# Moving the product with ones behind a burst's scores, in a group norm and attention kernel

## Chip, core and metric

The kernel runs on one core of one Trainium2 chip. The metric is the device time of one execution in microseconds, the median of a few runs. A profile is one further execution, recorded instruction by instruction.

## What is computed

The input x is 4 images of 512 channels and 48 by 48 = 2304 positions. The reference, cut to what matters:

```python
hn = _group_norm(x, gn_scale, gn_bias)                    # 32 groups of 16 channels
qkv = einsum('oc,bchw->bohw', qkv_w, hn) + qkv_b          # 1536 rows, then float16
q, k, v = ...                                             # 8 heads of 64 channels
w = softmax(einsum('bhct,bhcs->bhts', q * scale, k * scale), axis=-1)
a = einsum('bhts,bhcs->bhct', w, v)
return x + einsum('oc,bchw->bohw', proj_w, a) + proj_b
```

## The kernel before, in words

**Engines.** TensorE (PE) does all products, ScalarE (ACT) the exponentials, VectorE (DVE) evacuates PSUM and adds up the exponentials, GpSimd (POOL) divides by the sums, SyncE (SP) issues nearly all DMAs. Each works through its instructions in the order in which the program issues them, and the program fixes that order by hand: the loop at line 1355 calls small functions, and each call puts its instructions at the end of the queues of the engines concerned.

**Bursts and blocks.** Heads are worked in pairs, 4 pairs an image, 16 in all. A pair's 2304 query positions are cut into blocks: four of 512 and one of 256. A block against all 18 tiles of 128 key positions is cut into bursts of three exponential tiles (`stream`, line 935): 6 bursts for a block of 512, 3 for one of 256, so 27 a pair and 432 in all. There are 80 blocks, so 80 block ends.

**One burst, one turn of the loop.** In turn n the loop issues: the scores of burst n (`scores`, line 943: matmuls of k and q into a PSUM tile `ps`, and the exponential of each into `p`; there are three `ps` tiles, so a tile's scores wait for the exponential of the tile three before); the add of burst n-1's exponentials into `acc` (`add`, line 991; at a block's last burst two further adds fold the three thirds of `acc` into one); the values of burst n-2 (`values`, line 965: matmuls of v and p into `av`); and `fill` (line 1306).

**What fills the gaps.** `fill` issues work of other stages: statistics and normalization of the next image (`tasks`, on DVE), and pieces of chains (`beside`, on PE): chains for q and k (`pqk`, line 695), for v (`pv`, line 743) and for the output projection (`pr`, line 840). A planner gives each piece a cost and a due time, and a credit per turn decides how many are issued. All chains share one PSUM bank (`pw`), so a chain's first matmul waits until DVE has evacuated the chain before it.

**A block's end.** Let the block's last burst be e. In turn e+2, after `values` of e, DVE copies `av` to `avx` (line 989), and then comes `fill`. In turn e+3:

- loads that are due are issued (`loads`, a queue of functions with the turn from which they are due: stores of finished projections, the residual loads two chains ahead, and reloads of x for the next image, four tiles at a time; a projection or a reload queues them for the turn after);
- `add_up` (line 1015): two or four matmuls of `acc` with a tile of ones give the sums over keys, in the PSUM bank `sl`, which is the bank of `av` (one buffer), so they wait for the `avx` copy;
- `rows` (line 1044): DVE copies `sl` to `slx`, and SP issues two small DMAs that turn one row of each head into a tile of 128 partitions (`sums`);
- then `wanted` (line 1335), which issues pieces that the coming pair can't do without (and, if there are any, every load queued), the scores of n, the add of n-1, `fill`, and the values of e+1, whose `av` tile reuses the bank and so waits for the `slx` copy.

In turn e+4 POOL checks the sums' range (`check_sums`, line 1063), and DVE inverts them (`invert`, line 1073) after they have landed; SP sends the inverses to DRAM (`row`). In turn e+5 `spread` (line 1084) reads them back to all partitions (`ib`), and in turn e+6 POOL multiplies `avx` by `ib` into `att` (`divide`, line 1094).

The last blocks but one (`soon`, line 1349: two block ends) and the last block of all have lines of their own, from 1381 on. `load_x`'s DMA has line 512, `residual` line 811, a store line 876, the transfers of the sums line 1051. The conversion piece ahead of an image's first projection issues the first two residual loads itself, not through `loads` (`begin`, line 902).

Of the kernel before, what the change touches and what calls it, by code (L numbers as in the profile page):

```python
# [467 lines left out]
def fast_path(  # L468
# [312 lines left out]
    tasks, loads = deque(), deque()  # L781
# [161 lines left out]
    def scores(u):  # L943
        g, j, k, _ = u
        o, n = QBLOCKS[j]
        per = QB // n
        qt, kt = qk[g]
        pt = ppool.tile([P, BURST, 2, QB], F16, tag="p", name=f"p_{g}_{j}_{k}")
        for r in range(BURST):
            ps = ps_s.tile([P, 2, QB], F32, tag="ps", name=f"ps_{g}_{j}_{k}_{r}")  # L950
            for a in range(per):
                i = (k * BURST + r) * per + a
                for h in range(2):
                    rows = slice(h * D, (h + 1) * D)
                    nc.tensor.matmul(  # L955
                        ps[:, h, a * n : (a + 1) * n],
                        kt[rows, bass.ts(i, P)],
                        qt[rows, o : o + n],
                        start=True,
                        stop=True,  # L960
                    )
            nc.scalar.activation(pt[:, r], ps, AF.Exp)  # L962
        pts[u] = pt

    def values(u):
        g, j, k, last = u
        b, pr = divmod(g, NPAIR)
        o, n = QBLOCKS[j]
        per = QB // n
        pt = pts.pop(u)  # L970
        if k == 0:
            if j == 0:
                atts[g] = apool.tile([P, T], F16, tag="att", name=f"att_{g}")
            av[0] = ps_av.tile([P, QB], F32, tag="av", name=f"av_{g}_{j}")
        for r in range(BURST):
            for a in range(per):
                i = (k * BURST + r) * per + a
                for h in range(2):
                    lo = h * D
                    nc.tensor.matmul(  # L980
                        av[0][lo : lo + D, :n],
                        vv[b, pr // 2][:, i, pr % 2 * P + lo : pr % 2 * P + lo + D],
                        pt[:, r, h, a * n : (a + 1) * n],
                        start=(i == 0),
                        stop=(i == NT - 1),
                    )
        if last and u is not stream[-1]:
            avx[g, j] = work.tile([P, QB], F32, tag="avx", name=f"avx_{g}_{j}")
            nc.vector.tensor_copy(avx[g, j][:, :n], av[0][:, :n])  # L989

    def add(u):

        g, j, k, last = u
        pt = pts[u]
        if k == 0:
            acc[g, j] = [pt]
            return
        if j >= NQ - 2 and g == NG - 1 and (last or j == NQ - 1):
            acc[g, j].append(pt)
            return  # L1000
        before = acc[g, j][0]
        if k == 1:
            acc[g, j] = [
                work.tile(
                    [P, BURST, 2, QB], F16, tag="acc", bufs=1, name=f"acc_{g}_{j}"
                )
            ]
        t = acc[g, j][0]
        nc.vector.tensor_tensor(t, before, pt, ALU.add)  # L1009
        if last:  # L1010
            for r in range(1, BURST):
                nc.vector.tensor_tensor(t[:, 0], t[:, 0], t[:, r], ALU.add)  # L1012
            acc[g, j] = [t[:, :1]]

    def add_up(g, j, bank=None, more=False):


        o, n = QBLOCKS[j]
        per = QB // n
        sl = bank  # L1020
        if bank is None:
            sl = ps_av.tile([P, QB], F32, tag="av", name=f"sl_{g}_{j}")
        steps = [
            (t, r, a)
            for t in acc.pop((g, j))
            for r in range(t.shape[1])
            for a in range(per)
        ]
        for i, (t, r, a) in enumerate(steps):
            for h in range(2):  # L1030
                lo = h * D
                nc.tensor.matmul(  # L1032
                    sl[lo : lo + D, :n],
                    ones16,
                    t[:, r, h, a * n : (a + 1) * n],
                    start=(i == 0 and (g, j) not in open_sums),
                    stop=(i == len(steps) - 1 and not more),
                )
        if more:
            acc[g, j] = []  # L1040
            open_sums.add((g, j))
        return sl

    def rows(g, j, sl):

        o, n = QBLOCKS[j]
        sx = work.tile([P, QB], F32, tag="rows", name=f"slx_{g}_{j}")
        nc.vector.tensor_copy(sx[:, :n], sl[:, :n])  # L1048
        sm = small.tile([P, 2, QB // P], F32, tag="sums", name=f"sums_{g}_{j}")
        for h in range(2):  # L1050
            nc.sync.dma_start(sm[:, h, : n // P], sx[h * D : h * D + 1, :n])
        sums[g, j] = sm
        return sx
# [9 lines left out]
    def check_sums(g, j):  # L1063
        n = QBLOCKS[j][1]
        sm = sums[g, j][:, :, : n // P]
        ok = fine.rearrange("p (h i) -> p h i", h=2)[:, :, : n // P]
        for op, limit in ((ALU.is_ge, SUM_MIN), (ALU.is_le, SUM_MAX)):
            t = small.tile([P, 2, QB // P], F32, tag="in", name=f"in_{g}_{j}")
            t = t[:, :, : n // P]
            nc.gpsimd.tensor_scalar(t, sm, limit, None, op)  # L1070
            nc.gpsimd.tensor_tensor(ok, ok, t, ALU.mult)
# [234 lines left out]
    def fill(n):  # L1306

        idle = beside and beside[0][4] and not beside[0][4]()
        if ended(n - 1):
            room = 1.1 if idle else 0.0
        elif ended(n - BEHIND - 1):
            room = 1.1 if idle else 0.5
        else:
            room = 2.4 if idle else 1.1
        do_tasks(room)
        rate, work = 0.0, 0.0
        for us, _, _, _, _, _, need in beside:  # L1320
            work += us
            left = min(need * per_pair, len(stream) - 4) - n
            rate = max(rate, work / max(left, 1))
        credit[0] = min(credit[0] + rate, 4.0)
        closed = False
        while beside:
            us, _, first, last, when, after, _ = beside[0]
            if after > n or (first and closed) or (when and not when()):
                break
            if us > 0.1 and credit[0] < (0.0 if first and last else us / 2):  # L1330
                break
            issue()
            closed = closed or last

    def wanted(g):

        while any(p[6] <= g for p in beside):
            while loads:
                loads.popleft()[1]()
            while tasks:  # L1340
                tasks.popleft()[2]()
            issue()
            credit[0] = max(credit[0], 0.0)
# [7 lines left out]
    def block_at(n):  # L1351

        return stream[n][:2] if ended(n) and n not in soon else None

    for n in range(end):
        now[0] = n
        while loads and loads[0][0] <= n:
            loads.popleft()[1]()
        summed = block_at(n - BEHIND - 1)
        if summed:  # L1360
            rows(*summed, add_up(*summed))
        wanted(stream[n][0])
        scores(stream[n])
        if n > 0:
            add(stream[n - 1])
        if summed:

            fill(n)
        if n >= BEHIND:
            values(stream[n - BEHIND])  # L1370
        if block_at(n - BEHIND - 2):
            check_sums(*block_at(n - BEHIND - 2))
            invert(*block_at(n - BEHIND - 2))
        if block_at(n - BEHIND - 3):
            spread(*block_at(n - BEHIND - 3))
        if block_at(n - BEHIND - 4):

            divide(*block_at(n - BEHIND - 4))
        if not summed:
            fill(n)  # L1380
        if n - BEHIND in soon:
            g, j = stream[n - BEHIND][:2]
            sx = rows(g, j, add_up(g, j))
            if n - BEHIND == soon[1]:
                divide_here(g, j, sx, avx[g, j], nc.gpsimd)
        if n - BEHIND - 1 == soon[0]:
            check_sums(g, j)
            invert(g, j)
        if n - BEHIND - 2 == soon[0]:
            spread(g, j)  # L1390
            divide(g, j)
    g, b, j = NG - 1, B - 1, NQ - 1
    n = QBLOCKS[j][1]
# [142 lines left out]
```

## Time and profile before

| | |
|---|---|
| median of 3 runs | 1610.09 us (1609.6, 1610.09, 1612.28) |
| the profiled execution's own time | 1612.11 us |
| its span, first to last instruction | 1610.4 us |
| mean granted clock of PE | 0.997 |
| scores matmuls (line 955) | x2880, busy 356.6 us |
| values matmuls (line 980) | x2880, busy 361.5 us |
| chains of q and k (line 709) | x2464, busy 519.3 us |
| product with ones (line 1032, into sl) | x192, busy 31.0 us |
| exponentials (line 962) | x1296, mean 1025 ns |
| add of a burst (line 1009) | x270, mean 1795 ns |
| copy of sl to slx (line 1048) | x79, mean 633 ns |
| transfers of the sums (line 1051) | x158, median 2.1 us from issue to landing |

How to read the lines below: a group's line has the line of the kernel, the engine, the operation, what it writes <- what it reads, shapes and count; behind the first bar its busy time and the mean of one in ns; behind the second the engine's idle time just before its instructions and what ended it. A line in order of time begins with the start and the duration in us; instructions of one kind that follow each other are merged. "SPq" marks a DMA issue on SP. A matmul's shape "128*64" is the part of the array that it uses, rows by columns.

### The profile page before, as it was taken

Reading aid. Unit: us, or ns where it says so; the run is one execution under the profiler, and the core shown is the slowest. Engines: PE = TensorE matmul, PEld = TensorE weight load, DVE = VectorE, ACT = ScalarE, POOL = GpSimd, SP = SyncE. Lnnn points to the kernel's source line nnn. Section 1 sums busy time; section 2 is a strip of 40 time slices with the busy share of each in tenths; the row PEclk is TensorE's granted clock in tenths of the full one; section 3 lists DMA queues with packets and bytes.
Section 4 is the critical chain, followed back from the end, with each engine's and each line's share of the span. In section 5 each row is a group of like instructions: output and inputs, shape, how many; then the busy total and the mean of one; then the engine's idle time right before and its main releaser. Section 6 shows DMA issues by size and latency. Waiting matters only on the chain.

```text
span 1610.4 us, 28319 instructions
## 1 busy us (share of the span) xinstructions
PE 1582.2 (98%) x11500; PEld 694.0 (43%) x11500; DVE 1136.0 (71%) x1301; ACT 1267.1 (79%) x1360; POOL 318.9 (20%) x459
## 2 busy tenths in 40 slices
PE   7999999999999999999999999999999999999997
PEld 2533434443333534555333353355533334435554
DVE  6267668866666668986666666888666766667775
ACT  3077777888888888888887887877878888888895
POOL 1011102211121222322111121222112121222222
PEclk9999999999999999999999999999999999999999
DMA  7002020000000023511000001352100000016423
GB/s 218 5 14 66 12 65 23 18 14 11 14 18 14 9 70 119 155 53 28 14 11 18 14 12 52 99 160 83 25 14 18 14 15 11 15 31 190 123 66 127
DMA packets 94896, 82.10 MB, mean 51 GB/s; under 512 B 50852, under 2 KB 60964, under 8 KB 94756
## 3 DMA queue, kind: packets, MB, share of 16 engines
q1 hardware_dynamic: 92724, 78.35, 17.7%
q8 instruction: 92, 1.51, 0.4%
q10 hardware_dynamic: 1904, 1.84, 0.4%
q14 instruction: 48, 0.39, 0.1%
q0 software_dynamic: 128, 0.01, 0.0%
HBM read 60.70 MB, written 19.17 MB: 50 GB/s over the span
## 4 chain that ended last, share of the span: by engine, by line
PE 93%; DVE 2%; DMA 2%; issue 1%; ACT 1%; POOL 1%; SPq 0%; ACTq 0%; DVEq 0%; POOLq 0%
PE pqk L709 29%; PE ps L955 19%; PE av L980 19%; PE pv L760 16%; PE pr L844 8%; PE ps L709 1%; PE sl L1032 1%; DVE acc L1009 1%; ACT p L962 1%; DMA wqkv<-qkv_wT_dram 0%; DMA row<-inv 0%; DMA ib<-row 0%; POOL a L836 0%; DMA sums<-slx 0%; DVE r L871 0%
## 5 line engine op out<-in xcount | busy, mean ns | idle before, releaser
L962 ACT ACTIVATE p<-ps 128x1024 f16<-128x1024 f32 x1296 | 1233.4, 1025 | 312.3 <-PE ps L955 310.9
L1009 DVE TENSOR_TENSOR acc<-acc,p 128x3072 f16<-128x3072 f16 x270 | 484.6, 1795 | 70.8 <-ACT p L962 70.4
L709 PE MATMUL pqk<-x,wqkv 128*64 128x512 f32 (+1 forms) x2464 | 519.3, 551 | 0.0
L980 PE MATMUL av<-p,v 128*64 128x512 f16 (+1 forms) x2880 | 361.5, 364 | 0.4 <-DVE slx L1048 0.3
L955 PE MATMUL ps<-q,k 64*128 64x512 f16 (+1 forms) x2880 | 356.6, 358 | 1.2 <-ACT p L962 0.8
L760 PE MATMUL pv<-wqkv,x 128*64 128x256 f32 x2304 | 268.6, 380 | 0.0
L709 PEld LDWEIGHTS pqk<-x,wqkv 128*64 128x64 f32 x2464 | 168.9, 137 | 224.2 <-issue 166.8
L1070 POOL TENSOR_SCALAR in<-sums 128x8 f32<-128x8 f32 (+1 forms) x158 | 110.8, 702 | 718.5 <-DMA sums<-slx 712.0
L955 PEld LDWEIGHTS <-k 64*128 64x128 f16 x2880 | 106.1, 94 | 276.7 <-issue 228.1
L980 PEld LDWEIGHTS <-v 128*64 128x64 f16 x2880 | 132.1, 109 | 213.3 <-issue 169.1
L1096 POOL TENSOR_TENSOR att<-avx,ib 128x512 f16<-128x512 f32 (+1 forms) x78 | 121.9, 1563 | 445.6 <-DMA ib<-row 400.9
L760 PEld LDWEIGHTS pv<-wqkv,x 128*64 128x64 f32 x2304 | 160.1, 137 | 92.8 <-issue 4.5
L1009 DVE TENSOR_TENSOR acc<-p,p 128x3072 f16<-128x3072 f16 x79 | 138.1, 1748 | 0.0
L844 PE MATMUL pr<-a,whi 128*128 128x512 f32 (+1 forms) x311 | 122.2, 400 | 4.3 <-DVE q L719 2.3
L1012 DVE TENSOR_TENSOR acc<-acc 128x1024 f16<-128x1024 f16 x156 | 111.0, 712 | 5.3
L844 PE MATMUL pr<-a,wlo 128*128 128x512 f32 (+1 forms) x311 | 113.8, 373 | 0.0
L719 DVE TENSOR_SCALAR q<-pqk,bqkv 128x512 f16<-128x512 f32 (+1 forms) x79 | 54.9, 695 | 80.2 <-PE pqk L709 79.8
L719 DVE TENSOR_SCALAR k<-pqk,bqkv 128x512 f16<-128x512 f32 (+1 forms) x75 | 52.2, 696 | 77.9 <-PE pqk L709 77.6
L768 DVE TENSOR_TENSOR v<-pv,bv 128x512 f16<-128x512 f32 x72 | 49.7, 691 | 81.3 <-PE pv L760 81.1
L989 DVE COPY avx<-av 128x512 f32<-128x512 f32 (+1 forms) x79 | 50.6, 641 | 64.9 <-PE av L980 64.6
L871 DVE SCALAR_TENSOR_TENSOR r<-pr,bproj,r 128x512 f32<-128x512 f32 (+1 forms) x80 | 54.9, 694 | 44.0 <-PE pr L844 42.0
L844 PEld LDWEIGHTS pr<-a,whi 128*128 128x128 f32 x311 | 58.4, 188 | 43.6 <-issue 19.5
(79 smaller groups left out, 455.2 us busy)
## 6 DMA issues: line engine op xcount, KB each, us to landing
r<-x_dram SPq DMA_DIRECT2D x72, 256.0 KB, 3.2
out_dram<-r SPq DMA_DIRECT2D x69, 256.0 KB, 2.3
ib<-row SPq DMA_DIRECT2D x126, 128.0 KB, 3.1
x<-x_dram SPq DMA_DIRECT2D x62, 256.0 KB, 4.2
x<-x_dram SPq DMA_DIRECT2D x16, 128.0 KB, 4.8
sums<-slx SPq DMA_DIRECT2D x128, 2.0 KB, 2.1
ib<-row SPq DMA_DIRECT2D x30, 64.0 KB, 3.1
wqkv<-qkv_wT_dram SPq DMA_DIRECT2D x2, 768.0 KB, 7.0
```

Of the source, the lines that this page charges most:

```text
L709: nc.tensor.matmul(pw[0][lo : lo + D, :n], wqkv[:, c, w0 + lo : w0 + lo + D], hn[b, c, j], start=(c == 0), stop=(c == NC - 1),)
L719: nc.vector.tensor_scalar(qk[g][part][:, o : o + n], pw[0][:, :n], bqkv[:, col : col + 1], SCALE, ALU.add, ALU.mult,)
L760: nc.tensor.matmul(pw[0][lo : lo + D, a, :], hn[b, c, i * P // QB][:, at + lo : at + lo + D], wqkv[:, c, 2 * C + half * C // 2 :][:, : C / ...
L844: nc.tensor.matmul(ps[:, :n], w[:, c, bass.ts(m, P)], at32[b, j, c], start=(i == 0), stop=(i == len(steps) - 1),)
L871: nc.vector.scalar_tensor_tensor(xt[:, i], places[i], bias, xt[:, i], ALU.add, ALU.add)
L955: nc.tensor.matmul(ps[:, h, a * n : (a + 1) * n], kt[rows, bass.ts(i, P)], qt[rows, o : o + n], start=True, stop=True,)
L962: nc.scalar.activation(pt[:, r], ps, AF.Exp)
L980: nc.tensor.matmul(av[0][lo : lo + D, :n], vv[b, pr // 2][:, i, pr % 2 * P + lo : pr % 2 * P + lo + D], pt[:, r, h, a * n : (a + 1) * n], ...
L1009: nc.vector.tensor_tensor(t, before, pt, ALU.add)
L1012: nc.vector.tensor_tensor(t[:, 0], t[:, 0], t[:, r], ALU.add)
L1070: nc.gpsimd.tensor_scalar(t, sm, limit, None, op)
L1096: nc.gpsimd.tensor_tensor(atts[g][:, o : o + n], avx.pop((g, j))[:, :n], ibs.pop((g, j))[:, :n], ALU.mult,)
```

## The change

In a turn that handles a block's end, the product with ones, the `slx` copy and the two transfers of the sums are issued after the scores of the turn's burst instead of before them, and the loads that are due in that turn are issued after those transfers instead of first of all. In all other turns the order stays: due loads, wanted pieces, scores. The add of the burst before, `fill` and the values follow as before. `add_up`, `rows`, `wanted`, `scores` and the queue of loads are not changed.

```diff
+    def load_due(n):
+        while loads and loads[0][0] <= n:
+            loads.popleft()[1]()
+
     for n in range(end):
         now[0] = n
-        while loads and loads[0][0] <= n:
-            loads.popleft()[1]()
         summed = block_at(n - BEHIND - 1)
-        if summed:
-            rows(*summed, add_up(*summed))
+        if not summed:
+            load_due(n)
         wanted(stream[n][0])
         scores(stream[n])
+        if summed:
+
+            rows(*summed, add_up(*summed))
+            load_due(n)
         if n > 0:
             add(stream[n - 1])
         if summed:
```

More of the change, by code (lines that the diff above doesn't have):

```diff
@@ L1353, in block_at @@
         return stream[n][:2] if ended(n) and n not in soon else None
+    def load_due(n):
+        while loads and loads[0][0] <= n:
+            loads.popleft()[1]()
     for n in range(end):
         now[0] = n
-        while loads and loads[0][0] <= n:
-            loads.popleft()[1]()
         summed = block_at(n - BEHIND - 1)
+        if not summed:
+            load_due(n)
+        wanted(stream[n][0])
+        scores(stream[n])
         if summed:
             rows(*summed, add_up(*summed))
-        wanted(stream[n][0])
-        scores(stream[n])
+            load_due(n)
         if n > 0:
```

## Prediction

> **What bounds the kernel now.** I read the page first, then the groups of instructions by line, the waits, the order of time around block ends, and the stretches around the one hole that these showed.
>
> ```profile
> span 1610.4 us, 28319 instructions
> PE 1582.2 (98%) x11500; PEld 694.0 (43%) x11500; DVE 1136.0 (71%) x1301; ACT 1267.1 (79%) x1360; POOL 318.9 (20%) x459
> ```
>
> TensorE (PE) is busy for all but 28 us, 11.8 of which are one wait for the first load of x. The groups of PE, with the idle time ahead of each group after the last bar:
>
> ```profile
> L1032 PE MATMUL sl<-acc,ones 128*64 128x512 f16 (+1 forms) x192 | 31.0, 349 | 0.2 <-DVE avx L989 0.2
> L980 PE MATMUL av<-p,v 128*64 128x512 f16 (+1 forms) x2880 | 361.5, 364 | 0.4 <-DVE slx L1048 0.3
> L844 PE MATMUL pr<-a,whi 128*128 128x512 f32 (+1 forms) x311 | 122.2, 400 | 4.3 <-DVE q L719 2.3
> L1077 DVE RECIPROCAL inv<-sums 128x8 f32<-128x8 f32 (+1 forms) x78 | 14.8, 190 | 2.9 <-DMA sums<-slx 2.9
> ```
>
> So the product with ones (sl) waited 0.2 us in the whole run and the values behind it 0.4: moving sl has next to nothing to win where it stands. The two lines below say where something is lost: one wait of a projection (pr) of 2.3 us for VectorE (DVE), and one wait of VectorE's reciprocal of 2.9 us for the transfer of the sums. They are one event, seen in the order of time of SP and DVE:
>
> ```profile
> 1032.68 1.64 SPq L811 DMA_DIRECT2D r<-x_dram  x2
> 1034.41 1.80 SPq L512 DMA_DIRECT2D x<-x_dram  x4
> 1036.30 1.15 SPq L1051 DMA_DIRECT2D sums<-slx  x2
> ...
> 1041.19 0.18 DVE L1077 RECIPROCAL inv<-sums 128x4 f32<-128x4 f32 x1 [2.95 <-DMA sums<-slx]
> 1041.28 1.25 DVE L608 BATCH_NORM_STATS2 st<-x 128x6 f32<-128x512 f32 x2
> 1042.45 0.47 DVE L719 TENSOR_SCALAR q<-pqk,bqkv 128x256 f16<-128x256 f32 x1
> 1042.84 1.75 DVE L1009 TENSOR_TENSOR acc<-acc,p 128x3072 f16<-128x3072 f16 x1
> ```
>
> The slx copy ended at 1033.55, but its two transfers stand on SP behind four loads of x, leave at 1036.30 and land at 1041.1, behind those loads. DVE stands at inv; behind it on DVE is the evacuation of q, for which PE's next chain needs the only bank of chains. PE resumes at 1042.98. The stretches after it (PE busy, other engines, then PEclk, DMA share, GB/s):
>
> ```profile
> 1043.00:1044.40 1.40, 1.40 (x6) 1.18 (x7) 1.40 (x1) 0.00 (x0) 0.00 (x0) 1.00 0.19 55
> 1044.40:1048.00 3.60, 3.60 (x16) 1.01 (x14) 2.62 (x4) 1.89 (x3) 0.00 (x0) 0.53 0.54 111
> 1048.00:1052.00 4.00, 4.00 (x23) 2.19 (x22) 2.89 (x4) 2.35 (x4) 0.73 (x1) 1.00 0.55 184
> ```
>
> After the hole the clock was halved for 3.4 us.
>
> [...] 0.53 over 3.6 us right after a hole of 2.3 us, with no second case in the middle of the run. [...] the sums landed 0.8 us after the third x load (1040.09), not the usual 2.1 us after their issue. [...] six score matmuls (64*128) to the values (128*64) take 0.75 us start to start, six values to a chain of q or k in the same mode 0.67.
>
> **Part 1: sl behind the scores.** 77 of the 79 block ends go through the loop's branch that the diff edits; the last two but one have their own lines. Around each, PE does: values, chain X, [sl], scores, chain Y, values. After: values, X, scores, [sl], Y, values. No matmul is added. From the start times of single matmuls: q chain to sl 425 ns, sl to scores 312, scores to a chain 305, sum 1042; after, q chain to scores 525, scores to sl 305 (as scores to values), sl to chain 213 (as values to a chain; this pair isn't in the trace), sum 1043: **nothing**. For v chains 829 against 830. Where X is a projection (128*128) and Y is not, three changes of mode become two: 944 to 847 ns, in 2 places: **-0.2 us**. Projection to projection stays at three.
>
> What moves: the scores start 0.2 to 0.3 us earlier. They need the exponentials of the burst before; the tightest of the 77 had these done 0.56 us ahead, so no new wait. sl starts 0.85 us later (0.1 for the change of mode, 0.445 the scores, 0.305 to sl). Queued behind sl on PE is Y: sl's own inputs (acc, and the avx copy that frees its bank) are done by then, so it waits for nothing. On DVE the slx copy can start 0.42 us after sl, so at 1.27 us on the old scale; it used to start at 0.97 where it queued behind the evacuation of X and at 0.42 where it did not: **0.3 to 0.86 us later**. Cover: the values behind Y need the copied bank; they started 1.22 us (six projection matmuls) to 3.5 us after the copy's end. Less the shift, the least is 0.82 us: cost nothing. Without Y the cover would be gone: the one block end of the last ones without it had the values 0.05 us behind the copy and a wait of 0.42.
>
> Behind the copy on DVE stand the add of a burst (1.75), sometimes a task of the next batch's norm (0.4 to 0.7), then Y's evacuation, for which the next chain waits. I carried each block's shift down DVE's queue, taking off the idle gaps: where there is no task the gap of about 0.27 before Y's evacuation takes part, and the evacuation had 1.2 us to spare. With a task all 0.85 remain, against 0.7 to 1.0 us to spare; two blocks fall short, by 0.16 and 0.03: **+0.2 us**.
>
> **Part 2: due loads behind the sums.** Each end issues two sums transfers (0.59 us each) on SP; loads due then move behind them, so they wait for the copy and lie up to 2 us later. Only 11 ends have stores or loads due in that burst: ten in projection stages, and the one at 1036. In the ten, a residual load (r) lands about 2 us later (650.4 to 652.5 in the first), while the projection that adds it ends two bursts on, at 654: 1.5 us left, nothing. POOL's check of the sums waits for them in turn, but its casts of att come in other bursts.
>
> At 1036: the two r loads come from the conversion piece and stay in front; the sums may leave at 1034.4 (SP free; copy done at 1033.95), ahead of the four x loads, and land 2.1 to 3.3 us later, at 1036.5 to 1037.7. inv's turn on DVE is at 1038.7 (add started at 1036.3, plus 0.4 of shift, plus 1.98). **No wait.** Then two st (1.25) and q's evacuation (0.47) end at 1040.6. PE's values there start at 1039.85, the projection could follow at 1040.6: it waits some 0.1 instead of the 2.36 us by which its start was late: **-2.25 us** (bounds -1.3, if the sums land a us behind inv's turn, and -2.36). Without the hole the half clock should not come: half of 3.41 us is 1.7, the late starts that I can sum there are 1.46; I take **-1.6** (bounds 0 and -1.7). Late next is POOL's cast at 1524 (PE waits 1.1 us), untouched. The x loads land by about 1042; their statistics come three bursts on, past 1043.
>
> **Sum.** -0.2 + 0.2 - 2.25 - 1.6 = -3.85 us against the profiled execution: its own time is 1612.11 (span 1610.4 and 1.7 around it), giving 1608.3. The three runs are 1609.6, 1610.09 and 1612.28: two lie 2 to 2.5 us below the profiled one[...]. An execution of 1610.09 without it would lose only the 2.25: 1607.8. I take **1608.0**.
>
> **Rivals.**
> B, the transfers stay late: r loads, and x loads right behind, slow the sums so that inv still waits 1 us or more, or PE meets another hole there. For it: landing took 4.8 us before. Against: the traffic that delayed it is now behind it. 1609.3 to 1611, about 1610.
> C, slower: the way from sl to Y, which this trace doesn't have, costs a change of mode or a late weight load. Price 0.1 us at 77 ends, 7.7 us: 1608.0 + 7.7 = 1615.7. It decides from 0.07 us an end (5.3 us, past 1613.3). Against: values to a chain is the same pair of shapes and took 213 ns.
> D, the change doesn't do what it says at 1036: loads flushed by the demand for a pair's pieces come before the scores still. That demand acts at a pair's first burst and this is the third of pair 10; if I misread, 1610.
> E, more holes than this profile shows, in other executions, go too: about 1606.
>
> **Chances.** Likeliest case 0.64 (1606.6 to 1609.3), B and D 0.21, C 0.07, E 0.08. 0.2% is 3.2 us, about what a measurement of this kernel can tell from no change: faster means under 1606.87, slower over 1613.3. The likeliest case puts about a quarter of its chance below 1606.87, E all: faster 0.25, same 0.67, slower 0.08. Range 1606.0 to 1611.0: the likeliest case with both its bounds, B and D; C and half of E are left out.
>
> **What would show it.** Right: no wait of inv for the sums; no projection waiting for q at 1040; clock 1.00 there; sums at 1034.4 ahead of the x loads; scores to sl 305 and sl to chain 213 ns; waits of the values for slx below 1 us in all; DVE's wait of slx for sl up from 24.9 us, since it now reaches the copy before sl is done. Wrong: values waiting for slx at block ends, chains waiting for q, k, v at the tasks' blocks, r evacuations waiting for DMA, or a new hole with half clock.

## The result, and the profile after

| | before | changed |
|---|---|---|
| median of 22 runs each, one after the other on one chip | 1610.53 us (1608.33 to 1612.78) | 1608.53 us (1607.34 to 1610.56) |
| ratio | | 0.9988, 95% interval 0.9983 to 0.9994 |
| profiled execution, its own time | 1612.11 us | 1608.58 us |
| span | 1610.4 us | 1606.8 us |

So the change wins 1 to 2.7 us by the interval, 0.12% in the middle: within the 0.2% that the prediction called no change, and 0.5 us above the time it gave. The profiled execution of before was one of the longer ones, so the two profiles differ by more (3.5 us) than the medians (2.0).

The page after begins:

```profile
span 1606.8 us, 28320 instructions
PE 1579.1 (98%) x11500; PEld 691.7 (43%) x11500; DVE 1140.3 (71%) x1301; ACT 1267.1 (79%) x1360; POOL 329.5 (21%) x459
```

The groups that answer to those of before (idle time ahead of each behind the second bar):

```profile
L1032 PE MATMUL sl<-acc,ones 128*64 128x512 f16 (+1 forms) x192 | 32.6, 365 | 0.2 <-DVE avx L989 0.2
L980 PE MATMUL av<-p,v 128*64 128x512 f16 (+1 forms) x2880 | 360.8, 364 | 0.4 <-DVE slx L1048 0.3
L844 PE MATMUL pr<-a,whi 128*128 128x512 f32 (+1 forms) x311 | 122.0, 400 | 4.0 <-POOL a L836 2.2 <-DVE r L871 1.0 <-DVE q L719 0.6
L1077 DVE RECIPROCAL inv<-sums 128x8 f32<-128x8 f32 (+1 forms) x78 | 14.8, 190 | 1.4 <-DMA sums<-slx 1.4
L1048 DVE COPY slx<-sl 128x512 f32<-128x512 f32 (+1 forms) x79 | 50.6, 641 | 67.5 <-PE sl L1032 67.5
```

The product with ones and the values wait no more and no less than before. The projection's wait for q fell from 2.3 to 0.6 us, the reciprocal's wait for the sums from 2.9 to 1.4, and the copy's wait for sl rose from 24.9 to 67.5 us, which costs nothing by itself: DVE now stands ready before sl is done. The projection's waits for r rose from 0.2 to 1.0 us, and POOL's casts cost it 2.2 instead of 1.6.

The same place on SP, DVE and PE in the order of time, three answers:

```profile
1032.16 2.43 SPq L1089 DMA_DIRECT2D ib<-row  x2
1034.65 1.05 SPq L811 DMA_DIRECT2D r<-x_dram  x2
1035.80 1.14 SPq L1051 DMA_DIRECT2D sums<-slx  x2
1037.04 1.96 SPq L512 DMA_DIRECT2D x<-x_dram  x4
```

```profile
1036.55 1.75 DVE L1009 TENSOR_TENSOR acc<-acc,p 128x3072 f16<-128x3072 f16 x1
1039.45 0.18 DVE L1077 RECIPROCAL inv<-sums 128x4 f32<-128x4 f32 x1 [1.15 <-DMA sums<-slx]
1039.55 1.26 DVE L608 BATCH_NORM_STATS2 st<-x 128x6 f32<-128x512 f32 x2
1040.72 0.47 DVE L719 TENSOR_SCALAR q<-pqk,bqkv 128x256 f16<-128x256 f32 x1
```

```profile
1041.24 0.51 PE L844 MATMUL pr<-a,whi 128*128 128x512 f32 x1 [0.55 <-DVE q L719]
```

The sums now leave ahead of the four x loads, and land at 1039.4, 1.7 us earlier than before; inv still waits 1.15 us, and PE's hole is 0.6 us long. The stretches around it (PE busy, the other engines, then PEclk, DMA share, GB/s) show that the clock stays full:

```profile
1040.00:1041.30 1.30, 0.75 (x7) 0.17 (x3) 1.30 (x4) 1.30 (x2) 0.48 (x3) 1.00 0.92 299
1041.30:1048.00 6.70, 6.70 (x38) 3.72 (x40) 6.14 (x7) 4.68 (x6) 0.00 (x0) 1.00 0.58 142
```

Pair by pair (from one pair's first scores to the next pair's, for the last pair to its last scores; after against before), the trace says where the time went: pair 10, which holds that place, is 3.4 us shorter; nine others are 0.15 to 0.17 us shorter each; pairs 2, 5, 14 and 15 are 0.22, 0.73, 0.25 and 0.82 us **longer** (pairs 0 and 6 by under 0.1).

### The profile page after: what moved, and what is told of

It is laid out like the page before. It is cut to its first block, busy times and chain, and to the rows that moved or that the text cites. A ratio compares the mean times of both kernels' runs of the same rounds, so it can differ in the third digit from the quotient of the medians.

```text
span 1606.8 us, 28320 instructions
## 1 busy us (share of the span) xinstructions
PE 1579.1 (98%) x11500; PEld 691.7 (43%) x11500; DVE 1140.3 (71%) x1301; ACT 1267.1 (79%) x1360; POOL 329.5 (21%) x459
## 4 chain that ended last, share of the span: by engine, by line
PE 92%; DVE 3%; DMA 2%; ACT 1%; issue 1%; POOL 1%; SPq 0%; ACTq 0%; DVEq 0%; POOLq 0%
PE pqk L709 29%; PE ps L955 19%; PE av L980 19%; PE pv L760 15%; PE pr L844 7%; PE sl L1032 2%; PE ps L709 1%; ACT p L962 1%; DVE acc L1009 1%; DMA r<-x_dram 1%; DMA wqkv<-qkv_wT_dram 0%; DVE acc L1012 0%; DVE r L871 0%; DMA ib<-row 0%; POOL a L836 0%
## 5 line engine op out<-in xcount | busy, mean ns | idle before, releaser
L1070 POOL TENSOR_SCALAR in<-sums 128x8 f32<-128x8 f32 (+1 forms) x158 | 103.2, 653 | 724.7 <-DMA sums<-slx 718.0
L1096 POOL TENSOR_TENSOR att<-avx,ib 128x512 f16<-128x512 f32 (+1 forms) x78 | 125.3, 1607 | 436.9 <-DMA ib<-row 393.9
L1012 DVE TENSOR_TENSOR acc<-acc 128x1024 f16<-128x1024 f16 x156 | 116.3, 746 | 5.3
L1048 DVE COPY slx<-sl 128x512 f32<-128x512 f32 (+1 forms) x79 | 50.6, 641 | 67.5 <-PE sl L1032 67.5
```

The lines of the kernel that those rows point to most:

```text
L1096: nc.gpsimd.tensor_tensor(atts[g][:, o : o + n], avx.pop((g, j))[:, :n], ibs.pop((g, j))[:, :n], ALU.mult,)
```

## The experiments

Theory A was the prediction's: the one end near 1035, where loads of x stood ahead of the sums on SP, carries the gain, and the product's new place is about neutral. Rival B: the product's place wins. The expectations below use letters of their own (theory A, rivals B and C); they are not the rivals of the prediction. The first four kernels ran on one chip, each compared with the kernel before there (1610.05 us, 53 runs).

**Only the loads behind the sums.**

```diff
     for n in range(end):
         now[0] = n
-        while loads and loads[0][0] <= n:
-            loads.popleft()[1]()
         summed = block_at(n - BEHIND - 1)
         if summed:
             rows(*summed, add_up(*summed))
+        while loads and loads[0][0] <= n:
+            loads.popleft()[1]()
         wanted(stream[n][0])
```

> Only the order on SP changes: the due loads follow the transfers of the sums, while the product with ones and its copy stay ahead of the scores. Theory A (the gain is the one block end where x loads stood ahead of the sums): VectorE's wait of inv for the sums falls from 2.9 us to 1 us or less, the projection near 1041 waits under 0.7 us instead of 2.3, the clock stays full there; time about 2 us below before (1608 to 1609). Rival B (the gain comes from the new place of the product on TensorE): nothing of it is here, time as before (1610 to 1611), the turns around block ends on TensorE unchanged in both theories.

Measured: 1607.28 us, ratio 0.9983 (0.9975 to 0.9990). The profile has no wait of inv for the sums and no wait of a projection for q; pair 10 is 3.9 us shorter, and the pairs without projections are equal to before within 0.003 us. Rival B falls: all of the gain is here, without touching TensorE's order. The time is 0.7 us below the range expected.

**Only the product behind the scores.** Against the changed kernel:

```diff
-        if not summed:
-            load_due(n)
+        load_due(n)
         wanted(stream[n][0])
         scores(stream[n])
         if summed:
             rows(*summed, add_up(*summed))
-            load_due(n)
```

> Only the place of the product with ones, the copy and the transfers changes (behind the scores); due loads stay first of all. Theory A: the hole near 1041 stays (inv waits for the sums about 3 us, the projection about 2 us or more); TensorE takes 26 ns less at some 62 block ends (1.6 us), about given back by projections and chains that wait for VectorE; time 1609.5 to 1611. Rival B: most of the gain is here, 1608 to 1609.

Measured: 1611.51 us, ratio 1.0010 (1.0001 to 1.0018): slower than before, by a little, and above the range expected. Its waits, and the stretches around the place:

```profile
DVE inv L1077 <- DMA sums<-slx: 4.1, 1, 4.1
...
PE pr L844 <- DVE q L719: 3.5, 1, 3.5
```

```profile
1040.00:1043.50 3.50, 0.10 (x2) 0.00 (x0) 1.70 (x5) 1.85 (x3) 0.87 (x4) 0.97 0.19 39
1043.50:1047.00 3.50, 3.41 (x8) 2.51 (x8) 1.70 (x2) 0.00 (x0) 0.00 (x0) 0.54 0.29 44
```

The sums leave at 1037.2 instead of 1036.3, the hole grows from 2.3 to 3.5 us, and the half clock follows (0.54 over the next 3.5 us). The copy of this end is not what they wait for: it is done at 1033.4, while SP is busy with `ib`, r and x until 1037.1. What makes SP late is the copy of the block end before (below, under the hole). This is the change without its second half: the product's place alone makes the one bad place worse.

**The loads late at that one end.** A test in the loop of before, `late = summed == (9, NQ - 1)`: only there does `rows(*summed, add_up(*summed))` come ahead of the due loads.

> The kernel before with a single edit: at the last block end of pair 9, and nowhere else, the due loads follow the transfers of the sums. Theory A: as the run that moves the loads at all ends, within 0.5 us (1608 to 1609), since the ten other ends with due loads gain and lose nothing. Rival C (the sum of many small delays of the sums' transfers makes the gain): a tenth of the gain, time as before.

Measured: 1606.64 us, ratio 0.9981 (0.9973 to 0.9989). One end out of 80 gives all of it, more than expected; rival C (many small delays) falls. The ten other ends with due loads, which are all that separates this kernel from the first one, give nothing: with them the time was 0.64 us longer, which is within the scatter.

**The last two loads in front of the sums moved too.**

```diff
             if j == 0:
-                ahead(0)
-                ahead(1)
+                loads.append((now[0] + 1, lambda: ahead(0)))
+                loads.append((now[0] + 1, lambda: ahead(1)))
```

> The changed kernel, with the first two residual loads of each image queued as due loads, so that at the one end near 1035 they follow the sums too. Theory A: inv's wait of 1.15 us for the sums and the projection's wait of 0.6 us near 1041 go; 0.3 to 0.7 us below the changed kernel. Rival B: no difference from the changed kernel.

Measured: 1607.84 us, ratio 0.9987 (0.9980 to 0.9993), the changed kernel's own, measured apart, being 0.9988. Its profile has no wait of inv and none of a projection for q, as expected, but the time doesn't show the 0.5 us beyond the scatter; the interval is wider than the effect.

**The cover of the copy, taken away.** In the changed kernel, `sl = add_up(*summed)` stays behind the scores, and `rows(*summed, sl)` with the due loads goes behind `add(stream[n - 1])`.

> The changed kernel with the slx copy, its two transfers and the due loads issued behind the add of the burst before, so that the copy comes one add (1.67 us from start to start) later on VectorE. If the values behind a block's end have the cover that the trace of the changed kernel shows (from the copy's end to their start 0.79 to 2.8 us, median 0.83), 68 of the 77 ends wait, 0.9 us in most, 54 us in sum: about 1663 us. If the cover were hidden deeper (the matmuls' modelled ends or a longer queue), under 20 us.

Measured: 1672.57 us in two executions, ratio 1.0385 (1.0366 to 1.0404) to the kernel before on another chip than the runs above (1610.82 us, 14 runs). Its largest wait of PE:

```profile
PE av L980 <- DVE slx L1048: 49.3, 69, 0.9
```

69 ends wait, up to 0.9 us, as worked out from the copy's ends in the changed kernel's trace; projections that wait for r add 4.7 us, and some 10 of the 64 us above the changed kernel I didn't take apart. So the cover under the values (the time from the copy's end to their start) is about 0.8 us at most ends in the changed kernel; by the traces its median is 0.82 us, and was 1.70 before.

**Product behind the scores at all ends, loads late at one.** As the changed kernel, with `if summed != (9, NQ - 1): load_due(n)` ahead of the scores and `load_due(n)` behind the sums at that end only.

> The product with ones behind the scores at all ends, due loads first as before except at the last end of pair 9, where they follow the transfers. It differs from the run with loads late at that end alone only in the place of the product. Theory A: the hole near 1041 is 0.7 us or less; the place of the product by itself wins 26 ns at some 62 ends on TensorE and loses about as much or somewhat more in waits for VectorE: 1607 to 1608.5. Rival B (the place wins): below 1606.

Measured: 1606.53 us, ratio 0.9975 (0.9965 to 0.9985), on the chip of the last run and half a microsecond below the range expected.

**Product behind the scores only where DVE is free.**

```diff
         summed = block_at(n - BEHIND - 1)
+        early = summed and (len(tasks) > 0 or summed[0] in (5, 10, 14, 15))
```

At `early` ends the product stays ahead of the scores; the loads are late at the one end as above. 49 of the 77 products stand behind their scores.

> Due loads late only at the last end of pair 9, and the product behind the scores only at ends where VectorE has no statistics or normalization of the next image queued and no projections run (pairs 5, 10, 14 and 15 left out). Theory A: the 26 ns stay at some 45 ends (1.2 us) and the waits for VectorE at the busy ends go: 1605 to 1606.3, below the run with loads late at one end (1606.64). If the waits come at the free ends, no gain over it.

Measured: 1605.00 us, ratio 0.9966 (0.9954 to 0.9978): the best so far. In its profile pairs 2 and 5 are 0.09 and 0.13 us shorter than before, where the changed kernel had them 0.22 and 0.73 longer. In a second profile, below, pair 2 is 0.09 us shorter again, but pair 5 is 0.27 longer.

Since the last runs were on different chips, the four that matter ran again on one, in 13, 14, 15 and 6 executions (before: 1610.21 us, 37 runs).

> The changed kernel once more, on the same chip as the three runs beside it, so that they can be compared within one chip: 1608 to 1609, about 2 us below the kernel before.

> The kernel before with the due loads behind the sums at the one end alone, again. If that end carries the gain, 3 to 3.5 us below the kernel before, and about 1.5 us below the changed kernel.

> The product behind the scores at all ends, loads late at the one end alone, again. Against the run with loads late at the one end alone it gives the price of the product's place: between -0.5 and +0.5 us by the traces (26 ns won at the ends, waits for VectorE lost). Against the changed kernel it gives the price of the loads that are late at the ten other ends: 0 to 2 us.

> The product behind the scores only where VectorE is free, loads late at the one end alone, again: 1 to 1.5 us below the run with the loads alone, 5 us or so below the kernel before.

| | median us | ratio to before, 95% interval |
|---|---|---|
| changed kernel | 1607.17 | 0.9982 (0.9974 to 0.9991) |
| loads late at one end, product ahead | 1606.83 | 0.9979 (0.9971 to 0.9987) |
| loads late at one end, product behind everywhere | 1606.89 | 0.9981 (0.9974 to 0.9989) |
| loads late at one end, product behind where DVE is free | 1604.93 | 0.9970 (0.9957 to 0.9982) |

The changed kernel came out 1.4 us below its first measurement, more than its expectation allowed, so a difference of this size between two sets of runs says nothing. The second row was expected 1.5 us below the first and is 0.3 below. The second and third rows are the same: the product's place, taken at all ends, costs what it wins. The first row differs from the third by the loads at the ten other ends alone; they cost 0.3 us in these medians, not clear of the scatter. The fourth came out at 1604.9 to 1605.0 twice, 1.9 us below the second row: chosen by what DVE has to do, the product's place wins. At 49 ends the 26 ns found below make 1.3 us of it; the rest is not taken apart, and which part of the choice matters (no tasks queued, or no projections in the pair) was not tried.

## Why the prediction was right, point by point

**The hole: right in mechanism, too well by half a microsecond.** It was to shrink from 2.36 to 0.1 us and shrank to 0.62. The term that was off is the time at which the sums leave: 1034.4 by the prediction, 1035.80 measured. Two delays make up the 1.4 us: `ib`, ahead of them on SP, began 0.65 us later (1032.16 instead of 1031.51), and from its start to the end of the two r loads behind it passed 3.5 us instead of 2.8.

The first delay is the change's own doing, at the block end before. The prediction carried the copy's lateness down DVE's queue to the evacuations, but not to inv, on which `row`, then `ib`, then at this place the sums follow on SP. DVE before, then changed, at the fourth block end of pair 9:

```profile
1022.69 0.69 DVE L1048 COPY slx<-sl 128x512 f32<-128x512 f32 x1
...
1029.33 0.20 DVE L1077 RECIPROCAL inv<-sums 128x8 f32<-128x8 f32 x1
```

```profile
1023.57 0.69 DVE L1048 COPY slx<-sl 128x512 f32<-128x512 f32 x1 [0.86 <-PE sl L1032]
...
1030.22 0.20 DVE L1077 RECIPROCAL inv<-sums 128x8 f32<-128x8 f32 x1
```

The copy is 0.88 us later, and inv still 0.89. All profiles but that of the copy behind the add sort by where the product stands at that end. Counted from pair 10's first scores, this inv starts at 3.47 us in the six with the product ahead of the scores, and at 4.38 or 4.39 us in the six with it behind. Where the loads are late and the r loads in front, the sums leave at 8.3 to 8.7 us in the five with the product ahead (the forecast 1034.4 is 8.5), and the next inv doesn't wait; in the four with it behind they leave at 9.2 to 10.2, and inv waits 1.1 to 1.5 us in three of them. So the sums' time was right for the loads' half of the change alone.

The second delay looks like a long issue of `ib`, 2.43 us instead of 1.11. But before, the first r load behind it took 1.16 us, where it takes 0.58 behind the long `ib`. In all these twelve profiles one issue, the second of `ib` or the first of r, ends only 2.3 to 2.7 us after `ib` began. Where it is that of `ib`, both r loads still follow. What holds SP's issue there stays open.

The landing took 3.6 us from the first issue and 3.0 from the second; the prediction gave 2.1 to 3.3 from the time they leave. inv's turn came at 1038.3, close to the 1038.7 forecast.

**The half clock: right.** It was priced at 1.6 us and went. The bound of 1.7 is half of its length in the trace of before, 3.41 us (1044.48 to 1047.89). The price holds: in the five profiles without the hole and with the product ahead at this place, pair 10 is 3.7 to 3.9 us shorter, of which the hole is 2.3. The clock halved in the middle of both profiles with a hole of 2.3 us or more, and of none of the eleven others, whose hole there was 0.9 us at most; the wait of 1.6 us near 1521 in the changed kernel's profile didn't halve it either. That the hole brought it rests on these thirteen profiles. In that of before the clock stayed full for 1.50 us after PE had resumed (1042.98 to 1044.48); what sets this delay, or how long a hole it takes, is not shown.

In how many executions of before the clock halves is not shown. Of 53 runs of before on one chip, 30 had a mean clock of 0.997 and took 1610.32 us on average, 20 had 0.998 and took 1609.45; all 22 runs of the changed kernel had 0.998, all 13 of the product-only kernel 0.995 to 0.997. This fits the prediction's supposition that some executions halve the clock in the middle and others don't, an estimate from its three times, on which it took the median 2 us below the profiled execution. But the mean clock also holds a half clock at the end of each profile, where PE is almost idle: before, it lasts from 1604.26 us on, 6.1 us within the span, and PE is busy for 0.2 of the last 10.4 us. The second profile of the kernel with loads late at one end has 0.997 with no half clock in the middle (and 8.8 us of it at the end), the product-only kernel has 0.997 with one (and 5.4 us at the end). So the mean clock doesn't tell the two cases apart, and the two clusters that the first runs seemed to show are a continuous spread in 22.

**TensorE's order at block ends: "nothing" was 26 ns too much.** The nearest row stood in for a pair of kinds that the trace of before did not have. One end of before and the same end after, PE in order of time:

```profile
1198.94 0.38 PE L1032 MATMUL sl<-acc,ones 128*64 128x512 f16 x2
1199.25 0.82 PE L955 MATMUL ps<-q,k 64*128 64x512 f16 x6
1200.00 1.94 PE L709 MATMUL pqk<-x,wqkv 128*64 128x512 f32 x8
1201.77 0.82 PE L980 MATMUL av<-p,v 128*64 128x512 f16 x6
```

```profile
1195.52 0.82 PE L955 MATMUL ps<-q,k 64*128 64x512 f16 x6
1196.28 0.41 PE L1032 MATMUL sl<-acc,ones 128*64 128x512 f16 x2
1196.52 1.88 PE L709 MATMUL pqk<-x,wqkv 128*64 128x512 f32 x8
1198.23 0.81 PE L980 MATMUL av<-p,v 128*64 128x512 f16 x6
```

From sl to the chain it takes 237 ns, not 213. But a chain that follows the scores directly takes 1.77 us to the values, one that follows sl 1.72: behind the scores, which use the array in another shape (64*128), the chain's second pair of matmuls comes 51 ns later (480 ns after the first) than behind sl or the values (128*64, 429 ns). With sl between, the chain itself starts 24 ns later than behind the values. In sum 26 ns less at nearly every end without projections, 0.15 us a pair. This is a gain that the prediction did not have; its rival C, which made the same boundary dearer, had the sign wrong.

**DVE's lateness: right in kind, too small.** The prediction found two ends where the tasks of the next image leave too little, 0.16 and 0.03 us. The first is there (the chain at 278.9 starts 0.27 us late); the second isn't. That the product's place causes such waits shows best in pair 2: it is 0.17 to 0.45 us longer in the six profiles with the product behind the scores everywhere (that of the copy behind the add left out), and equal in the three where only loads move. Missed were inv's lateness, told above, and places where another cause adds to it: an add that folds `acc` while POOL divides. In the changed kernel, DVE and then POOL:

```profile
598.65 2.37 DVE L1012 TENSOR_TENSOR acc<-acc 128x1024 f16<-128x1024 f16 x2
600.94 0.74 DVE L719 TENSOR_SCALAR q<-pqk,bqkv 128x512 f16<-128x512 f32 x1
```

```profile
597.55 2.19 POOL L1096 TENSOR_TENSOR att<-avx,ib 128x512 f16<-128x512 f32 x1 [7.07 <-DMA ib<-row]
```

The two folds take 1.42 us where POOL is idle. Here, and near 641, 1486 and 1519, they take 2.1 to 2.4, each time beside a POOL divide or cast. The evacuation behind them is late, and PE starts its next chain 0.3 to 0.6 us late; near 1521 it waits for POOL's own cast, 1.6 us instead of 1.0. Before, the divides began at other points (at 596.0 for this one). The folds' mean rose from 712 to 746 ns, and to 727 in a second profile. That the divide moved because the sums land later is likely, since it waits for the last transfer of their chain, but it was not tried by itself. The same overlaps come and go from profile to profile: pair 15 was 0.8 us longer than before in the first profile of the changed kernel and 0.6 shorter in the second, and pair 14 was 0.25 us longer in two profiles where only loads move, as it is here, so its overlap can't be put down to the product.

**The sum.** Predicted 3.85 us against the profiled execution, 3.53 measured; 1608.0 against 1608.53. At the one place 3.85 us were forecast and pair 10 is 3.4 shorter. The two errors of the product's place (26 ns an end won, about as much lost in waits) cancelled, so the sum is better than its terms, and that it came so close is in part luck.

**Rivals.** B (the transfers stay late) came true for 1.15 of 2.95 us of inv's wait, which is past the 1 us that the prediction gave as its sign, but the time stayed below B's range. C, D and E did not come. Of the signs of being right, the full clock, the values' small waits for slx and DVE's longer wait for sl came as forecast; no wait of inv, no projection waiting for q, sums at 1034.4 and 213 ns from sl to the chain did not.

## What to carry to other kernels

When the bound engine has almost no idle time, a reordering can only win at the few places where it has: list those waits first, and try the edit at one of them alone before making it a rule. Here one line at one of 80 block ends gives the whole gain of the change, and the product's new place is worth something only at chosen ends; that DVE's room is what counts there is likely, not shown. A small transfer that a waiting chain needs belongs ahead of bulk loads in its queue: behind four of them the sums left 1.9 us after SP was free for them, and the first took 4.6 us to land instead of the usual 2.1. And when an instruction is moved, follow its lateness along every queue that it feeds: here 0.9 us on a copy came back a block later as the wait of the transfers that the change was to hasten.

## What the runs showed that I had not expected

- From the scores (64*128) to an f32 chain of q or k (128*64) the gap at the change was not all that was lost: the chain's second pair of matmuls came 480 ns after the first instead of 429, too. With two short f16 matmuls (128*64) between them it was 429, and a block end took 26 ns less in all.
- A fold of f16 tiles on DVE took 0.69 us in each of the 139 cases of the changed kernel's trace without a POOL divide or cast of note beside it (in 30 of them one of POOL's small range checks ran beside it, and they took 0.69 us as well), and 0.98 to 1.67 us in the 15 with one.
- At the start pairs of matmuls come every 0.85 us, later every 0.43. That the first is a half clock is an estimate from the pace alone; it ended anywhere from 15.4 to 18.0 us in these profiles, and the first scores start at 76.2 to 77.1 us: nearly a microsecond of scatter from run to run that no edit made.
